# Two edits in the attention layers of a conv-attention hybrid: a product with the identity made a transpose, and four row products made one transpose and a masked product

## The chip, the cores and the metric

The kernel runs on one core of one Trainium2 chip. The metric is the device time of one execution in microseconds (us); the time given is the median of several runs. Beside the runs there is one profiled execution, whose trace gives the start and the duration of each instruction on each engine: PE is TensorE (matrix products; PEld is its separate load of the stationary operand), DVE is VectorE, ACT is ScalarE, POOL is GpSimd, SP is SyncE, which issues the DMAs.

## The reference, cut to what matters

The whole network has four layers on `x` of 2 x 56 x 56 x 128. Layers 0 and 1 are convolutions with selective scans. Layers 2 and 3 work on 2 x 3136 tokens of 128 channels: layer 2 is an attention without weights of its own and a mixer of long convolutions, layer 3 an attention with weights and 64 experts. The change touches the two attentions:

```python
def _L2_attn_ref(q):
    sim = jnp.einsum('blh,bmh->blm', q, q) * scale
    sim = jnp.where(diag[None, :, :], jnp.float32(-1000000000.0), sim)
    attn = jax.nn.softmax(sim, axis=-1)
    return jnp.einsum('blm,bmh->blh', attn, q)

def _L3_attn_ref(x, Wq, bq, Wk, bk, Wv, bv):
    q = jnp.einsum('bnf,of->bno', x, Wq) + bq
    k = jnp.einsum('bnf,of->bno', x, Wk) + bk
    v = jnp.einsum('bnf,of->bno', x, Wv) + bv
    scores = jnp.einsum('bnf,bmf->bnm', q, k) / TEMP
    alpha = jax.nn.softmax(scores, axis=-1)
    return jnp.einsum('bnm,bmf->bnf', alpha, v)

t = t + _L2_attn_ref(_ln_t(t))
t = t + _L2_ffn_ref(_ln_t(t), ...)      # the mixer
t = t + _L3_attn_ref(_ln_t(t), ...)
t = t + _L3_ffn_ref(_ln_t(t), ...)      # the experts
```

## The kernel before, in words

`program` (L2174) runs the layers one after the other: layer 0, layer 1, attention 2, the mixer, attention 3, the experts. The token tensor `X` stays in SBUF through layers 2 and 3, with 112 tokens to a partition tile.

Both attentions run in `Attend.run` (L1198). A chunk is 448 queries of one image; there are 7 chunks per image, 14 in all. A chunk goes over 25 key tiles of 128 keys (the last has 64). Per key tile `j`:

- PE forms the scores of 128 keys and 448 queries (L1219, into a PSUM pool of three banks called "sc");
- ACT takes the exponential into `e` (L1221, a pool of six);
- POOL adds `e` up in `total` (L1230, L1232), whose column sums are the softmax denominators;
- PE adds values times `e` into the accumulator `av` (L1213). This runs two key tiles behind the scores: `waiting` holds up to three tiles.

At the end of a chunk DVE copies the accumulator to `by` (L1244), channels on the partitions and 448 queries along the row. For each of four groups of 112 queries PE multiplies `by` by `out_w` (L1248), which turns the group to tokens on the partitions, and multiplies `total` by a column of ones (L1251), which gives the denominators. DVE takes the reciprocal (L1255) and adds the scaled result to `X` (L1258). In attention 3 `out_w` is the value weight matrix; in attention 2 there is no such matrix, and `out_w` is the identity. All of these are float32.

During the chunks of attention 2, `also` (L1301) puts in steps that prepare the mixer's input for the chunk before: a layernorm after tile 4 (`layernorm_tokens`, L71, on DVE, ACT and POOL), its transposes after tile 11 (L1566), and products after tiles 14 and 18 (L1578, L1595). During attention 3 it puts in the second image's layernorm, transposes and keys (L1403, L1417, L1428), and the experts' layernorm and gate products (L1930, L1934).

In attention 3 the exponent needs a shift per query, about the largest score. `Queries` (L1118) makes the next chunk's queries while the current chunk runs. `begin` (L1132), at tile 0, projects the queries into `q` and keeps a bfloat16 copy `q16`. `some` (L1146), after each tile, does two more of 28 low-precision score products (L1154, bank pool "lo" of two) and takes each one's row maximum on DVE (L1158), so that all are done by tile 15. Then it finishes:

- DVE takes the largest of seven maxima per query, negated: `m`, 112 x 4 (L1161);
- PE turns each of the four columns of `m` into a row of 112 by a product with the identity (L1164), all into one partition of one "pr" bank: 1 x 448;
- ACT copies that row to a bfloat16 row `shift` (L1169);
- PE multiplies it by `part`, one row of 1/128, which spreads the shift over the 128 channels of a second "pr" bank (L1171; the pool has one bank, so the first must be read before);
- DVE adds it to `q` (L1172).

The query vectors then carry the shift in themselves, and the next chunk's first score product needs the shifted `q` (`take`). The first chunk's queries are made ahead of the loop, in `Attention3.run` (L1348), spread over the steps that prepare the first image's keys.

The order of instructions on each engine is not written out by hand: the program is recorded in the order of the calls, and a scheduler of the language orders each engine's instructions and puts the semaphore waits. Each engine runs its own list in order.

Of the kernel before, what the change touches and what calls it, by code (L numbers as in the profile page):

```python
# [15 lines left out]
BF16 = mybir.dt.bfloat16  # L16
AF = mybir.ActivationFunctionType
ALU = mybir.AluOpType
# [7 lines left out]
TP = 112  # L26
NT = L // TP
CH = 448
# [6 lines left out]
class Chip:  # L35


    def __init__(self, ctx, tc):
        self.tc, self.nc = tc, tc.nc
        nc = tc.nc  # L40
        const = ctx.enter_context(tc.tile_pool(name="const", bufs=1))
        self.ident = const.tile([128, 128], F32, name="ident")
        make_identity(nc, self.ident)
        self.eps = const.tile([128, 1], F32, name="eps")
        nc.gpsimd.memset(self.eps, 1e-5)
        self.one = const.tile([128, 1], F32, name="one")
        nc.gpsimd.memset(self.one, 1.0)
        self.ones = const.tile([1, 128], F32, name="ones")
        nc.gpsimd.memset(self.ones, 1.0)
        self.X = const.tile([TP, NT, B, C], F32, name="X")  # L50
        self._turn = 0
# [59 lines left out]
class Scans:  # L111
# [201 lines left out]
    def run(self):  # L313
        with ExitStack() as ctx:
            self.open(ctx)
            with self.k.tc.manual_schedule():
                self.all_steps()
# [795 lines left out]
def four(ps):  # L1113

    return ps[:TP].rearrange("p (i c) -> p i c", c=C)


class Queries:  # L1118
# [6 lines left out]
    def __init__(self, k, keys, low, weights, bias, sp, banks):  # L1125
        self.k, self.keys, self.low, self.weights, self.bias, self.sp = k, keys, low, weights, bias, sp
        self.banks = banks
        self.part = sp.tile([1, 128], BF16, name="part")
        k.nc.gpsimd.memset(self.part, 1.0 / C)
        self.todo = []  # L1130

# [14 lines left out]
    def some(self, left):  # L1146

        nc = self.k.nc
        if len(self.todo) <= left:
            return  # L1150
        while len(self.todo) > left:
            c, i = self.todo.pop(0)
            ps = self.banks("lo")[:TP, 0:CH]
            nc.tensor.matmul(  # L1154
                ps, lhsT=self.q16[:, TP * i : TP * (i + 1)], rhs=self.low[self.b][:, CH * c : CH * (c + 1)],
                start=True, stop=True,
            )
            nc.vector.tensor_reduce(self.m[:, i, c : c + 1], ps, AX.X, ALU.max)  # L1158
        if not self.todo:
            m = self.sp.tile([TP, 4], F32, name="mm")  # L1160
            nc.vector.tensor_reduce(m, self.m, AX.X, ALU.max, negate=True)  # L1161
            ps = self.banks("pr")
            for i in range(4):
                nc.tensor.matmul(  # L1164
                    ps[0:1, TP * i : TP * (i + 1)], lhsT=m[:, i : i + 1], rhs=self.k.ident[:TP, :TP],
                    start=True, stop=True,
                )
            row = self.sp.tile([1, CH], BF16, name="shift")
            nc.scalar.copy(row, ps[0:1, 0:CH])  # L1169
            ps = self.banks("pr")[:, 0:CH]  # L1170
            nc.tensor.matmul(ps, lhsT=self.part, rhs=row, start=True, stop=True)  # L1171
            nc.vector.tensor_tensor(self.q, self.q, ps, ALU.add)  # L1172
# [6 lines left out]
class Attend:  # L1179
# [18 lines left out]
    def run(self, keys, queries, V, scale, out_w, skip=None, also=lambda at, j: None):  # L1198

        k, nc, X = self.k, self.k.nc, self.k.X  # L1200
        made = isinstance(queries, Queries)
        chunks = [(b, qc) for b in range(B) for qc in range(NCH)]
        for at, (b, qc) in enumerate(chunks):
            if made:
                q = queries.take()
            else:
                q = queries[b][:, CH * qc : CH * (qc + 1)]
            av = self.bank("av")
            acc = av[:, 0:CH]
            total = self.ep.tile([KT, CH], F32, name="total")  # L1210

            def weigh(j, n, e):
                nc.tensor.matmul(acc, lhsT=V[b][:n, j, :], rhs=e[:n], start=j == 0, stop=j == NKT - 1)  # L1213

            waiting, first = [], None
            for j in range(NKT):
                n = min(KT, L - KT * j)
                ps = self.bank("sc")[:, 0:CH]
                nc.tensor.matmul(ps[:n], lhsT=keys[b][:, KT * j : KT * j + n], rhs=q, start=True, stop=True)  # L1219
                e = self.sp.tile([KT, CH], F32, name="e")  # L1220
                nc.scalar.activation(e[:n], ps[:n], AF.Exp, scale=scale)  # L1221
                if skip is not None:
                    c0, c1 = max(KT * j, CH * qc), min(KT * j + n, CH * (qc + 1))
                    if c0 < c1:
                        own = e[:n, c0 - CH * qc : c1 - CH * qc]
                        nc.vector.tensor_tensor(own, own, skip[:n, c0 - KT * j : c1 - KT * j], ALU.mult)
                if j == 0:
                    first = e
                elif j == 1:
                    nc.gpsimd.tensor_tensor(total, first, e, ALU.add)  # L1230
                else:
                    nc.gpsimd.tensor_tensor(total[:n], total[:n], e[:n], ALU.add)  # L1232
                if made and at + 1 < len(chunks):
                    if j == 0:
                        queries.begin(*chunks[at + 1])
                    queries.some(max(0, 30 - 2 * j))
                waiting.append((j, n, e))
                if len(waiting) > 2:
                    weigh(*waiting.pop(0))
                also(at, j)  # L1240
            for one in waiting:
                weigh(*one)
            by = self.ep.tile([128, CH], F32, name="by")
            nc.vector.tensor_copy(by, acc)  # L1244
            pt = four(self.bank("pr"))
            pd = av[:TP, CH : CH + 4]
            for i in range(4):
                nc.tensor.matmul(  # L1248
                    pt[:, i, :], lhsT=by[:, TP * i : TP * (i + 1)], rhs=out_w, start=True, stop=True
                )  # L1250
                nc.tensor.matmul(  # L1251
                    pd[:, i : i + 1], lhsT=total[:, TP * i : TP * (i + 1)], rhs=self.ones, start=True, stop=True
                )
            r = self.ep.tile([TP, 4], F32, name="r")
            nc.vector.reciprocal(r, pd)  # L1255
            for i in range(4):
                xo = X[:, 4 * qc + i, b, :]
                nc.vector.scalar_tensor_tensor(xo, pt[:, i, :], r[:, i : i + 1], xo, ALU.mult, ALU.add)  # L1258


class Attention2:
# [30 lines left out]
    def run(self, early, inputs):  # L1292

        k = self.k
        done = early()
        with k.pool("a2") as sp, ExitStack() as ctx:
            skip = sp.tile([KT, KT], F32, name="skip")
            k.nc.vector.tensor_scalar(skip, k.ident, -1.0, 1.0, ALU.mult, ALU.add)
            att = Attend(k, ctx)

            def also(at, j):  # L1301
                steps = {4: inputs.tokens, 11: inputs.channels, 14: inputs.blocks, 18: inputs.direct}
                if at > 0 and j in steps:
                    steps[j](lambda: att.bank("lo"), *divmod(at - 1, NCH))

            att.run(self.uT, self.uT, self.V, 128.0**-0.5, k.ident, skip=skip, also=also)
            for step in (inputs.tokens, inputs.channels, inputs.blocks, inputs.direct):
                step(lambda: att.bank("lo"), B - 1, NCH - 1)
        return done
# [910 lines left out]
```

## Time and profile before

| what | us |
|---|---|
| median of 3 runs | 8835.18 |
| lowest and highest run | 8833.89, 8835.39 |
| the profiled execution: its own time | 8835.43 |
| its span, from first to last instruction | 8833.6 |
| first score product of attention 2 in its loop, last result product | 5758.4, 6360.4 |
| first tokens step of attention 3 (L1403) | 7883.8 |
| first score product of attention 3 (L1219), last result product | 7949.6, 8645.2 |

So layers 0 and 1 take the first 65% of the span, attention 2 about 600 us, the mixer about 1520, attention 3 about 760 with its preparation, the experts the last 190. Three score products of attention 2 stand earlier, at 5686, beside the end of layer 1.

How to read the views: the page's first part gives the busy time of each engine; a busy time over the whole span is a mean over stages with different limits, so stretches are asked for by themselves. A matrix product of float32 shows as two records ("x2" for one instruction of the program), a transpose and a bfloat16 product as one. In a timeline a line gives the start in us, the length in us, engine, line, operation, output and inputs, the number of records merged, and in brackets the idle time of that engine ahead of it with what ended it. In a list of waits the columns are the total in us, the times, and the longest.

### The profile page before, as it was taken

To read this page: it belongs to the slowest core of one execution; us is meant where nothing else is said; L and a number is where in the kernel's file an instruction comes from. 1 tells how busy PE (TensorE), PEld (TensorE's weight loads), DVE (VectorE), ACT (ScalarE), POOL (GpSimd) and SP (SyncE) were. 2 spreads that over 40 slices of the span, in tenths; PEclk is the share of its full clock that TensorE was granted. 3 is DMA by queue.
4 is the path that set the end of the run, shared out by engine and by line. 5 is a ranking of instruction groups with operands and counts; after the bars stand their busy time and mean duration, and the time that the engine had idled before them with its cause. 6 is when DMAs were issued, how large, how long until landed. Compare 5 with 4: busy or idle time off the path is not lost. (4 is left out here: it accounts for less than half of the span.)

```text
span 8833.6 us, 103494 instructions
## 1 busy us (share of the span) xinstructions
PE 8003.9 (91%) x31559; PEld 4877.1 (55%) x31559; DVE 6756.2 (76%) x7017; ACT 5217.6 (59%) x11166; POOL 6844.0 (77%) x4232
## 2 busy tenths in 40 slices
PE   8999999999998888888888888699989989989998
PEld 4555555555554444444444444345578878875555
DVE  8999998999987997998899799821266676665442
ACT  6888876888876776776777677533322222214331
POOL 5999986999986996998799699666577767756551
PEclk9999999999998999999899899799999999989999
DMA  4676654667654884885688488320133333320004
GB/s 145 217 218 213 211 186 128 217 217 213 211 179 109 221 219 118 215 223 161 173 224 216 116 224 219 93 34 3 30 98 106 103 93 106 104 56 8 15 1 139
DMA packets 846617, 1276.69 MB, mean 145 GB/s; under 512 B 182813, under 2 KB 504350, under 8 KB 846058
## 3 DMA queue, kind: packets, MB, share of 16 engines
q1 hardware_dynamic: 846058, 1270.07, 50.7%
q8 instruction: 249, 4.08, 0.2%
q14 instruction: 310, 2.54, 0.1%
HBM read 1230.00 MB, written 46.58 MB: 145 GB/s over the span
## 5 line engine op out<-in xcount | busy, mean ns | idle before, releaser
L495 POOL TENSOR_TENSOR p<-h,c 128x784 f32<-128x784 f32 x2048 | 3763.7, 1864 | 291.8 <-DVE h L401 146.0
L401 DVE TENSOR_TENSOR_SCAN h<-a,state,h 128x784 f32<-128x784 f32 x1200 | 2169.9, 1833 | 2.5 <-ACT a L381 1.6
L421 PE MATMUL acc<-p,center 128*128 128x392 f32 x4096 | 1496.8, 501 | 6.5 <-POOL p L495 6.3
L421 PE MATMUL acc<-p,ident 128*128 128x392 f32 x4096 | 1429.5, 493 | 0.5 <-POOL p L495 0.4
L479 DVE TENSOR_TENSOR h<-du,b 128x784 f32<-128x784 f32 x1152 | 1096.5, 952 | 229.7 <-PE b L407 212.5
L381 ACT ACTIVATE a<-delta,L1A 128x784 f32<-128x784 f32 x896 | 819.8, 915 | 425.0 <-DVE h L401 418.6
L421 PEld LDWEIGHTS acc<-p,ident 128*128 128x128 f32 x4096 | 747.6, 190 | 533.4 <-issue 33.4
L421 PEld LDWEIGHTS acc<-p,center 128*128 128x128 f32 x4096 | 743.0, 193 | 497.1 <-issue 25.0
L1232 POOL TENSOR_TENSOR total<-total,e 128x448 f32<-128x448 f32 (+1 forms) x644 | 734.6, 1141 | 329.1 <-ACT e L1221 289.6
L498 POOL TENSOR_TENSOR h<-du,b 128x784 f32<-128x784 f32 x448 | 831.7, 1857 | 0.0
L1221 ACT ACTIVATE e<-sc 128x448 f32<-128x448 f32 (+1 forms) x700 | 376.9, 542 | 722.8 <-PE sc L1219 594.6
L407 PE MATMUL b<-three,sel 96*128 96x512 bf16 (+1 forms) x2304 | 587.0, 336 | 174.0 <-DVE h L479 102.0
L381 ACT ACTIVATE a<-delta,L0A 128x784 f32<-128x784 f32 x704 | 643.3, 914 | 169.7 <-DVE h L401 165.2
L401 DVE TENSOR_TENSOR_SCAN h<-a,h 128x784 f32<-128x784 f32 x400 | 702.6, 1774 | 3.5 <-ACT a L381 3.1
L359 ACT ACTIVATE X<-X,BT 112x128 f32<-112x128 f32 x2100 | 683.8, 391 | 0.2
L1736 POOL TENSOR_TENSOR u<-u,T 128x1024 f32<-128x1024 f32 x192 | 448.6, 2358 | 265.9 <-DVE u L1734 265.7
L401 DVE TENSOR_TENSOR_SCAN h<-h,state,a 128x784 f32<-128x784 f32 x336 | 618.0, 1839 | 0.0
L1720 ACT ACTIVATE less<-cv 128x512 f32<-128x512 f32 x256 | 152.1, 595 | 612.2 <-PE cv L1698 586.9
L407 PEld LDWEIGHTS <-sel 96*128 96x128 bf16 x2304 | 225.0, 101 | 521.3 <-issue 365.5
L359 ACT ACTIVATE big<-big,BT 112x64 f32<-112x64 f32 x1680 | 444.6, 335 | 0.0
L1732 ACT ACTIVATE T<-T 128x1024 f32<-128x1024 f32 x128 | 135.2, 1056 | 407.4 <-DVE T L1730 279.2
L1837 PE MATMUL pj<-u,Wm 128*128 128x196 f32 (+8 forms) x1536 | 355.6, 385 | 21.2 <-POOL u L1756 11.1
(541 smaller groups left out, 14336.4 us busy)
## 6 DMA issues: line engine op xcount, KB each, us to landing
c<-rows SPq DMA_DIRECT2D x1024, 392.0 KB, 4.0
c<-rows SPq DMA_DIRECT2D x2048, 196.0 KB, 4.0
b<-rows SPq DMA_DIRECT2D x512, 196.0 KB, 4.6
b<-rows SPq DMA_DIRECT2D x192, 392.0 KB, 4.6
wA<-win SPq DMA_DIRECT2D x64, 448.0 KB, 3.9
wB<-win SPq DMA_DIRECT2D x64, 448.0 KB, 6.2
wC<-win SPq DMA_DIRECT2D x64, 448.0 KB, 4.7
wD<-win SPq DMA_DIRECT2D x64, 448.0 KB, 3.8
```

Of the source, the lines that this page charges most:

```text
L359: self.k.nc.scalar.activation(x["bT"][:, i, c0:c1], g["duT"][x["ci"]][:, i, c0:c1], AF.Copy, scale=g["BT"][:, r : r + 1])
L381: self.k.nc.scalar.activation(x["a"], g["delta"][ci], AF.Exp, scale=self.w["A"](g["kd"], ci, x["n"]))
L401: self.k.nc.vector.tensor_tensor_scan(h, a, b, start, ALU.mult, ALU.add)
L407: self.k.nc.tensor.matmul(ps[:, c0:c1], lhsT=self.w["selB"](x["n"]), rhs=x["g"]["three"][:, c0:c1], start=True, stop=True)
L421: nc.tensor.matmul(job["acc"][:, i, 0:392], lhsT=self.w["sum"], rhs=x["p"][:, 392 * i : 392 * (i + 1)], start=False, stop=n == NS - 1,)
L479: nc.vector.tensor_tensor(one["h"], one["g"]["du"][one["ci"]], one["b"], ALU.mult)
L495: nc.gpsimd.tensor_tensor(now["p"], now["h"], now["c"], ALU.mult)
L498: nc.gpsimd.tensor_tensor(three["h"], three["g"]["du"][three["ci"]], three["b"], ALU.mult)
L1221: nc.scalar.activation(e[:n], ps[:n], AF.Exp, scale=scale)
L1232: nc.gpsimd.tensor_tensor(total[:n], total[:n], e[:n], ALU.add)
L1736: nc.gpsimd.tensor_tensor(u[:, :, :, o], u[:, :, :, o], half, ALU.add)
L1837: nc.tensor.matmul(ps[:, lo - c0 : hi - c0], lhsT=Ws[f][:, eo, 3 - r, :], rhs=u[:, b, f, lo - a0 : hi - a0], start=f == 0, stop=f == 1,)
```

## The change

Two edits.

- In `Attend.run`, `out_w` may now be None, and attention 2 passes None instead of the identity. The result is then turned to tokens by `nc.tensor.transpose` with the identity as the moving operand, and not by a float32 product with it. Attention 3 keeps its product with the value weights.
- In `Queries.some`, the four products that lay the columns of `m` into one row become one transpose of `m` (112 x 4) into four rows of 112. One DVE tensor_tensor then multiplies these four rows, each repeated four times along the row, by the 4 x 4 corner of the identity, each element repeated 112 times. The result `shift` is 4 x 448 in bfloat16: row `i` holds its own 112 values at place `i` and zeros elsewhere. `part` gets four rows of 1/128 instead of one, so the spreading product (now with four partitions instead of one) adds the four rows up to the same 448 values. ACT's copy is gone.

```diff
@@ class Queries: __init__
-        self.part = sp.tile([1, 128], BF16, name="part")
+        self.part = sp.tile([4, 128], BF16, name="part")
         k.nc.gpsimd.memset(self.part, 1.0 / C)
@@ Queries.some
             m = self.sp.tile([TP, 4], F32, name="mm")
             nc.vector.tensor_reduce(m, self.m, AX.X, ALU.max, negate=True)
-            ps = self.banks("pr")
-            for i in range(4):
-                nc.tensor.matmul(
-                    ps[0:1, TP * i : TP * (i + 1)], lhsT=m[:, i : i + 1], rhs=self.k.ident[:TP, :TP],
-                    start=True, stop=True,
-                )
-            row = self.sp.tile([1, CH], BF16, name="shift")
-            nc.scalar.copy(row, ps[0:1, 0:CH])
+            ps = self.banks("pr")[0:4, 0:TP]
+            nc.tensor.transpose(ps, m, self.k.ident[:TP, :TP])
+            row = self.sp.tile([4, CH], BF16, name="shift")
+            shape = [4, 4, TP]
+            nc.vector.tensor_tensor(
+                row.rearrange("p (i c) -> p i c", c=TP), ps.unsqueeze(1).to_broadcast(shape),
+                self.k.ident[0:4, 0:4].unsqueeze(2).to_broadcast(shape), ALU.mult,
+            )
             ps = self.banks("pr")[:, 0:CH]
             nc.tensor.matmul(ps, lhsT=self.part, rhs=row, start=True, stop=True)
             nc.vector.tensor_tensor(self.q, self.q, ps, ALU.add)
@@ Attend.run
             for i in range(4):
-                nc.tensor.matmul(
-                    pt[:, i, :], lhsT=by[:, TP * i : TP * (i + 1)], rhs=out_w, start=True, stop=True
-                )
+                if out_w is None:
+                    nc.tensor.transpose(pt[:, i, :], by[:, TP * i : TP * (i + 1)], k.ident)
+                else:
+                    nc.tensor.matmul(
+                        pt[:, i, :], lhsT=by[:, TP * i : TP * (i + 1)], rhs=out_w, start=True, stop=True
+                    )
                 nc.tensor.matmul(
                     pd[:, i : i + 1], lhsT=total[:, TP * i : TP * (i + 1)], rhs=self.ones, start=True, stop=True
                 )
@@ Attention2.run
-            att.run(self.uT, self.uT, self.V, 128.0**-0.5, k.ident, skip=skip, also=also)
+            att.run(self.uT, self.uT, self.V, 128.0**-0.5, None, skip=skip, also=also)
```

Line numbers from L1162 on are up to three higher in the changed kernel.

## The prediction

> **What bounds the kernel now.** I read the page's first part, then busy time by stretch, then TensorE's waits, then the timeline at the two places that the diff touches. The page puts TensorE first, and the stretches say where that matters: attention 2 lies at 5759 to 6361 us, the loop of attention 3 at 7949 to 8646.
>
> ```profile
> PE 8003.9 (91%) x31559; PEld 4877.1 (55%) x31559; DVE 6756.2 (76%) x7017; ACT 5217.6 (59%) x11166; POOL 6844.0 (77%) x4232
> ...
> core 0: us, PE busy (x) PEld busy (x) DVE busy (x) ACT busy (x) POOL busy (x), PEclk, DMA share, GB/s
> 5759.00:6361.00 602.00, 601.13 (x1830) 311.18 (x1828) 106.96 (x249) 236.19 (x423) 395.92 (x349) 1.00 0.06 11
> 7949.00:8303.00 354.00, 347.17 (x1174) 180.32 (x1173) 184.06 (x343) 155.38 (x254) 214.75 (x193) 1.00 0.03 10
> 8306.00:8646.00 340.00, 337.92 (x1106) 174.89 (x1104) 146.34 (x283) 130.49 (x222) 200.15 (x177) 1.00 0.01 5
> ```
>
> In both stretches PE is busy 98 to 100% at the full granted clock (1.00), DMA is nearly idle, and no other engine passes 66%. TensorE's waits inside attention 3's loop say the same:
>
> ```profile
> PE lo L1154 <- DVE m L1158: 6.8, 21, 0.6
> PE pr L1248 <- DVE by L1244: 0.7, 1, 0.7
> PE pr L1417 <- POOL U L86: 0.5, 3, 0.2
> ```
>
> A PE microsecond here is therefore a microsecond of the end, if nothing else becomes late. In the timeline, take distances between starts of weight loads, since ends of matmuls are modelled. The end of an attention 2 chunk:
>
> ```profile
> 5798.74 0.28 PEld L1248 LDWEIGHTS pr<-ident,by 128*112 128x112 f32 x2
> 5798.95 0.29 PEld L1251 LDWEIGHTS av<-onecol,total 128*112 128x112 f32 x2
> 5799.16 0.28 PEld L1248 LDWEIGHTS pr<-ident,by 128*112 128x112 f32 x2
> ```
>
> Each float32 product is two passes ("x2"): 0.21 us for a result product, 0.21 for a row-sum product, 0.42 for a pair. A float32 transpose of the same shape already stands in the kernel, at L1403, and is one pass; four of them take 8028.92 to 8029.36, 0.11 us each:
>
> ```profile
> 8028.92 0.60 PE L1403 MATMUL pr<-ident,A 128*112 128x128 f32 x4
> 8029.25 0.30 PEld L1219 LDWEIGHTS sc<-q,first 128*128 128x128 f32 x2
> 8029.36 0.92 PE L1219 MATMUL sc<-q,first 128*128 128x448 f32 x2
> ```
>
> And the maxima of a later chunk of attention 3: eight passes, a value product, the spreading product L1171, DVE's addition.
>
> ```profile
> 8142.18 0.18 DVE L1161 TENSOR_REDUCE mm<-m 112x4 f32<-112x28 f32 x1
> 8142.57 0.66 PEld L1164 LDWEIGHTS pr<-ident,mm 112*1 112x1 f32 x8 [0.65 <-issue]
> 8143.43 0.30 PEld L1213 LDWEIGHTS av<-e,first 128*128 128x128 f32 x2 [0.20 <-ACT e L1221]
> 8143.53 0.52 ACT L1169 CAST shift<-pr 1x448 bf16<-1x448 f32 x1 [0.25 <-PE pr L1164]
> 8144.38 0.09 PEld L1171 LDWEIGHTS <-part 1*128 1x128 bf16 x1 [0.65 <-issue]
> 8144.78 0.62 DVE L1172 TENSOR_TENSOR q<-q,pr 128x448 f32<-128x448 f32 x1 [2.42 <-PE pr L1171]
> ```
>
> From 8142.57 to 8143.43 is 0.86 us for eight passes, 0.107 each.
>
> **What the Trainium skill says.** "TensorE: Matmul & The Clock Gate", section Terms, calls the transpose mode four times faster for float32. This trace shows only half the time (0.11 against 0.21), and I use the trace. "Perfetto Trace Analysis", section Transposes, advises a transpose instead of a standard matmul; the same rows agree. "VectorE: DVE Perf Modes", section on the TRN2 errata, prices a float32 tensor_tensor at (N+151)/0.96 ns, 624 ns for 448 elements; L1172 with 448 elements and one operand in PSUM took 621, so it agrees. The TensorE page's Part 1 says that the PE runs at half clock until a window of about 3.4 us has been busy; here the stretch 7940 to 7946 shows a granted clock of 0.50, and 7948 to 7950 shows 1.00.
>
> **The change part by part.**
>
> *Attention 2's results (14 chunks, 4 each).* Each product of two passes (0.21) becomes one transposed pass of L1403's shape (0.11): 0.10 saved, 4 x 14 x 0.10 = 5.6 us. Bounds: nothing, if the alternation with the row sums sets the pace; 5.9, if the pass costs as little as half the pair, 0.105. The addition to the tokens waits for the row sums, which come after the same passes, so the normalization and the next steps on DVE, ACT and POOL start 0.4 us earlier too: nothing takes PE's place as the late one. `total` was complete at 5796.14, 2.4 us before its product.
>
> *Attention 3's maxima, 13 times in the loop.* Four products (eight passes, 0.86 us) become one transpose with 4 stationary columns and 112 moving ones. The nearest rows are the transposes with 112 moving columns (L1566: 6247.46 to 6247.85, four, 0.10 each). Saved 0.86 - 0.10 = 0.76 us; 13 x 0.76 = 9.9 us. Bounds: 8.6, if the single transpose takes 0.2, and 10.4, if it takes 0.06.
>
> *ACT's copy of the row goes to DVE.* ACT loses 14 x 0.52 us; ACT is 38 to 44% busy in the loop, so I count nothing. DVE gains 14 tensor_tensor of 4x448 with an operand in PSUM: 0.62 each by L1172. Bounds 0.47 (448 elements with no fixed part) and 2.0 (four cycles an element, if the two broadcasts slow it). What hides it: in the built order of the changed program, L1171 stands after a value and a score product (2 x 0.75 us) in every chunk of the loop; in the later chunks it stood after one before. The row needs 0.11 (PE's end to DVE's start, as at L1172) + 0.62 + 0.21 (DVE's mm end 8142.36 to L1164's start 8142.57) = 0.94 us. So L1171 does not wait, by 0.56 us. If the cover were gone, it would cost 0.94 x 13 = 12 us. Behind a waiting L1171 on PE stand the next score and value products; behind the row on DVE stand the reciprocal L84 and the addition L1172. In the chunks with a normalization in flight (three of the loop) L84 waits for ACT's root, which ends at 8036.90 in the second of them, while the row would run at about 8035.7 to 8036.3: nothing. `U` is then complete at 8038.29 and its transpose L1417 comes at 8039.78 now, 0.76 earlier after: still 0.7 us to spare.
>
> *The first maxima, ahead of the loop.* Here the chain is exposed and the PE clock is half: L1164 from 7946.40, ACT's copy from 7947.97, L1171 from 7948.54, the addition from 7948.93, first score product 7949.60. After: one pass, done by about 7946.75; DVE's row 7946.85 to 7947.47; its cast of q (0.39) to 7947.86, L1171 meanwhile; addition from about 7948.0 to 7948.6; score product 7948.65, some 0.95 earlier. One low-precision score product (0.19) moves from ahead of it to behind it. I take 0.7. Bounds: 1.0, and a loss of 1.0, if the thinner PE work leaves the clock at half for one more window (3.4 us at half speed is 1.7 lost).
>
> *Moves without a price.* In the seventh chunk of attention 2 the built order puts the first L1566 transpose five tiles earlier, just where PE stands still for an exponential (6067.27 to 6067.52); its input is done at 6066.94. Zero, at most 0.3. `part` gets three more rows: one memset. SP's queue is untouched.
>
> Sum: 5.6 + 9.9 + 0.7 = 16.2 us. The profiled execution took 8835.43 (span 8833.6 and 1.8 around it): 8835.4 - 16.2 = 8819.2. The median is 0.25 lower, so 8819.0, 0.18% less. About 0.2% (17.7 us) is what a measurement of this kernel can tell from no change, so the forecast is a real gain that just misses it.
>
> **The rivals.**
> - *More than counted* (8816): each L1164 and L1171 also shows some 0.1 to 0.2 us between the end of the passes before it and its own first pass, because its load was not pulled ahead. If one of these goes per chunk, 13 x 0.2 = 2.6 us more. For it: the row is ready half a microsecond before L1171's turn, so its load may go ahead. Against it: the load stood exposed before as well, though the copy was done 0.3 us earlier.
> - *The transposes of results gain nothing* (8824.6): the pace of 0.104 per pass is as near to a weight load of 112 columns as to a stream of 128, and alternating modes may cost what the pass saves. Against it: L1403 and L1566 stand between normal products with no gap over 0.03 us.
> - *Attention 3's gain turns into waits* (8829, only 5.6 + 0.7 left): PE comes 0.76 us earlier to exponentials or to `U`. Against it: value products lag by two tiles, and the spare time above.
> - *Slower, by the row on DVE* (8841): the row of 4x448 with two stride-0 operands takes d. Above d = 1.2 us (1.5 less 0.32) L1171 stops PE at all 13 places, and from d = 2.4 (16.2/13 more) the whole change loses. At d = 2.85, 13 x 1.65 = 21.5 lost, less 16.2, is +5. Against it: broadcast operands in L80 (512 elements, 0.69) run at an element per cycle.
>
> **How the numbers follow.** Forecast as summed, 8817 to 8821.5: 0.62. More than counted: 0.18. No gain in attention 2: 0.08. Waits: 0.08. Slower: 0.04. The range 8814 to 8826 takes in the first three with their bounds (0.88, of which some spills over). Faster by over 0.2% (below 8817.5): the second case and a tail of the first, 0.25. Slower by over 0.2% would need d of about 3.8 us or an unforeseen stall: 0.03. Within: 0.72.
>
> **What would show it.** In the profile after: L1248's line in attention 2 with 56 records instead of 112 and 0.32 us from pair to pair; one record in place of L1164's eight and 0.1 us between its load and the next product's; a DVE row of about 0.62 us and no PE wait on it; the stretches of attention 2 and of the loop of attention 3 shorter by 5.6 and 9.9 us, others as before. PE waiting at L1171 for DVE, or a row above 1.2 us, would show it wrong; so would mixer or expert stages that change length.

## The result and the profile after

The changed kernel takes 8815.5 us (median of 12 runs, 8808.65 to 8821.97), the kernel before 8834.42 in the same comparison (12 runs, 8825.94 to 8845.55): a ratio of 0.9979 [0.9972, 0.9987] (in brackets, here and below, a 95% interval), 18.9 us less. The forecast was 16.2 us less, 8819.0.

The profiled execution of the changed kernel was the longest of its twelve, 8821.97 us with a span of 8820.2. Its span is only 13.4 us shorter than the profiled span before, so spans must be compared by stage. The stages below are cut at starts of products that both programs have: first value product of attention 2, last row sum of attention 2, first tokens step of attention 3 (L1403, now L1406), first and last score product of attention 3's loop, end of the span.

| stage, us | before | after | difference |
|---|---|---|---|
| up to attention 2 | 5760.1 | 5758.3 | -1.8 |
| attention 2 | 600.6 | 592.8 | -7.8 |
| mixer | 1523.5 | 1524.1 | +0.6 |
| attention 3, preparation | 65.4 | 64.7 | -0.7 |
| attention 3, loop | 690.4 | 680.0 | -10.4 |
| experts, end | 193.6 | 200.3 | +6.7 |

The three stages with an edit in them got 18.9 us shorter. The experts got 6.7 longer though nothing in them was edited, which was not expected and is taken up below.

First the same views as before. The page's first part and the busy time of the stretches of the changed kernel (attention 2, and the two halves of attention 3's loop; after the comma the busy time and records of PE, PEld, DVE, ACT, POOL, then the granted clock):

```profile
PE 7989.4 (91%) x31405; PEld 4864.6 (55%) x31405; DVE 6764.6 (77%) x7031; ACT 5212.6 (59%) x11152; POOL 6843.2 (78%) x4232
```

```profile
core 0: us, PE busy (x) PEld busy (x) DVE busy (x) ACT busy (x) POOL busy (x), PEclk, DMA share, GB/s
5757.40:6350.80 593.40, 592.68 (x1769) 302.41 (x1768) 106.96 (x247) 236.34 (x423) 396.68 (x349) 1.00 0.07 11
7939.89:8280.00 340.11, 333.52 (x1104) 173.19 (x1104) 188.45 (x350) 147.93 (x240) 209.23 (x188) 1.00 0.03 8
8280.00:8619.90 339.90, 338.81 (x1070) 174.01 (x1069) 148.89 (x283) 130.67 (x222) 205.87 (x182) 1.00 0.02 7
```

PE has 154 records fewer: 56 in attention 2 and 14 times seven in attention 3. DVE has 14 more, ACT 14 fewer. PE is still busy 98 to 100% of the three stretches, and no other engine took its place. TensorE's waits in attention 3's loop are those of before, to the tenth of a microsecond:

```profile
PE lo L1154 <- DVE m L1158: 6.8, 21, 0.6
PE pr L1251 <- DVE by L1244: 0.7, 1, 0.7
PE pr L1420 <- POOL U L86: 0.5, 3, 0.2
```

There is no wait at the spreading product (L1171) for DVE's new row. The three new groups, by line (duration in ns: least, median, most):

```profile
L1249 PEld LDWEIGHTS pr<-ident,by x56: 132/203/207, 5796.4 to 6350.8; 128*112 128x112 f32 x56
...
L1163 PE MATMUL pr<-ident,mm x14: 256/256/391, 7937.6 to 8566.3; 112*4 112x112 f32 x14
...
L1166 DVE TENSOR_TENSOR shift<-pr,ident x14: 612/612/614, 7938.0 to 8566.6; 4x448 bf16<-4x448 f32 x14
```

The row on DVE takes 612 ns, the same each time. The end of an attention 2 chunk, in the weight loads of the changed kernel:

```profile
5796.44 0.14 PEld L1249 LDWEIGHTS pr<-ident,by 128*112 128x112 f32 x1 [0.19 <-issue]
...
5796.95 0.21 PEld L1249 LDWEIGHTS pr<-ident,by 128*112 128x112 f32 x1
5797.05 0.32 PEld L1254 LDWEIGHTS av<-onecol,total 128*112 128x112 f32 x2
5797.22 0.20 PEld L1249 LDWEIGHTS pr<-ident,by 128*112 128x112 f32 x1
5797.31 0.31 PEld L1254 LDWEIGHTS av<-onecol,total 128*112 128x112 f32 x2
5797.48 0.20 PEld L1249 LDWEIGHTS pr<-ident,by 128*112 128x112 f32 x1
...
5797.81 0.30 PEld L1219 LDWEIGHTS sc<-big 128*128 128x128 f32 x2
```

From transpose to transpose it is 0.27, 0.26 us (5796.95, 5797.22, 5797.48), where a pair took 0.42. From the first load of the block to the load of the next score product it is 1.37 us; before it was 1.94:

```profile
5798.05 0.18 PEld L1248 LDWEIGHTS pr<-ident,by 128*112 128x112 f32 x1 [0.19 <-issue]
...
5799.99 0.30 PEld L1219 LDWEIGHTS sc<-big 128*128 128x128 f32 x2
```

That is 0.57 less per chunk, and 14 x 0.57 = 8.0, which is the stage's difference to 0.2 us.

The maxima of a chunk of attention 3, PE's records. Before:

```profile
8141.73 0.92 PE L1219 MATMUL sc<-q,first 128*128 128x448 f32 x2
8142.57 0.93 PE L1164 MATMUL pr<-ident,mm 112*1 112x112 f32 x8
8143.43 1.02 PE L1213 MATMUL av<-e,first 128*128 128x448 f32 x2
```

After, with DVE's row and the spreading product in another view of the same stretch:

```profile
8130.78 0.92 PE L1219 MATMUL sc<-q,first 128*128 128x448 f32 x2
8131.56 0.26 PE L1163 MATMUL pr<-ident,mm 112*4 112x112 f32 x1
8131.65 0.93 PE L1213 MATMUL av<-e,first 128*128 128x448 f32 x2
```

```profile
8131.85 0.61 DVE L1166 TENSOR_TENSOR shift<-pr,ident 4x448 bf16<-4x448 f32 x1 [0.44 <-PE pr L1163]
8132.42 0.92 PE L1219 MATMUL sc<-q,first 128*128 128x448 f32 x2
8133.26 0.09 PEld L1171 LDWEIGHTS <-part 4*128 4x128 bf16 x1 [0.65 <-issue]
```

From the start of the score product to the end of the value product behind the block it was 2.72 us (8141.73 to 8144.45) and is 1.80 (8130.78 to 8132.58): 0.92 less, against a forecast of 0.76. The row is done at 8132.46, and L1171 comes 0.8 us later. DVE is off PE's path.

Last, the start of the loop. Before, its first two score products (four passes) took 1.77 us:

```profile
7949.60 1.77 PE L1219 MATMUL sc<-q,first 128*128 128x448 f32 x4 [0.28 <-DVE q L1172]
```

After, the same four passes:

```profile
7939.89 3.20 PE L1219 MATMUL sc<-q,first 128*128 128x448 f32 x4
```

They run at half clock: the changed kernel enters the loop before TensorE's clock has come up, and gives back 3.20 - 1.77 = 1.43 us inside the loop.

### The profile page after: what moved, and what is told of

It reads as the page before. It is cut to its first block, busy times and chain, and to the rows that moved or that the text cites. A ratio compares the mean times of both kernels' runs of the same rounds, so it can differ in the third digit from the quotient of the medians.

```text
span 8820.2 us, 103186 instructions
## 1 busy us (share of the span) xinstructions
PE 7989.4 (91%) x31405; PEld 4864.6 (55%) x31405; DVE 6764.6 (77%) x7031; ACT 5212.6 (59%) x11152; POOL 6843.2 (78%) x4232
## 6 DMA issues: line engine op xcount, KB each, us to landing
c<-rows SPq DMA_DIRECT2D x2048, 196.0 KB, 4.1
b<-rows SPq DMA_DIRECT2D x512, 196.0 KB, 4.6
```

## The experiments

Four questions were open: whether the two edits act only in their own stages; why the end got 6.7 us longer; why a pair in attention 2 fell by 0.15 us where the price taken gave 0.10; and why a block in attention 3 fell by 0.92 where 0.76 was counted. All kernels were compared with the kernel before on the same chip. Their stages:

| stage, us | attention 2 | preparation | loop | end |
|---|---|---|---|---|
| before | 600.6 | 65.4 | 690.4 | 193.6 |
| after | 592.8 | 64.7 | 680.0 | 200.3 |
| attention 2's edit alone | 592.7 | 65.7 | 690.5 | 200.3 |
| attention 3's edit alone | 601.0 | 64.7 | 679.9 | 194.9 |
| the change again | 592.3 | 64.6 | 680.0 | 194.9 |
| transposes grouped | 594.4 | 64.7 | 680.0 | 194.8 |
| four transposes in attention 3 | 593.1 | 65.5 | 683.5 | 200.0 |
| row made three times | 592.4 | 66.8 | 680.3 | 193.3 |
| extra products at the end | 592.5 | 64.6 | 680.1 | 196.0 |
| extra products in two places | 593.2 | 65.4 | 678.6 | 195.0 |

In the grouped kernel the last row sums stand eight passes in a row, and its stage is cut at the last of them. The expectations of attention 2's edit alone, attention 3's edit alone, the change again and the grouped kernel count attention 2 from its first score product, 1.6 us ahead of the first value product: their 602.2 us are 600.6 in this table, and their 594.4, 596.6 and 597.2 are 592.8, 595.0 and 595.6.

### Attention 2's edit alone

The kernel before, with `out_w` None in attention 2.

```diff
-                nc.tensor.matmul(
-                    pt[:, i, :], lhsT=by[:, TP * i : TP * (i + 1)], rhs=out_w, start=True, stop=True
-                )
+                if out_w is None:
+                    nc.tensor.transpose(pt[:, i, :], by[:, TP * i : TP * (i + 1)], k.ident)
...
-            att.run(self.uT, self.uT, self.V, 128.0**-0.5, k.ident, skip=skip, also=also)
+            att.run(self.uT, self.uT, self.V, 128.0**-0.5, None, skip=skip, also=also)
```

> Attention 2's edit alone (results turned by transposes); attention 3's maxima as before. Theory T (a transposed pass costs about 0.05 us of PE when it stands between normal passes, a quarter of the two passes of the product, so a pair falls from 0.415 to 0.264 us): attention 2 from its first loop score product to its last row sum takes 594.4 us instead of 602.2, and the loop of attention 3 stays at 690.4. The whole kernel is 7.8 us faster than before, give or take the clock of the experts' start. Rival P (the prediction's size, 0.10 us saved per result): 596.6 us and 5.6 us.

Measured: 8831.53 us (13 runs, 8827.92 to 8841.52), ratio 0.9997 [0.9989, 1.0005]. Attention 2 took 592.7, the loop 690.5, the end 200.3. The stage falls by 7.9, which is theory T's size and not the prediction's (592.8 and 595.0 in the table's cut), and no other edited stage moves. Theory T's size was worked out after the first profile, so this repeats a measurement; it doesn't show what a single transposed pass costs. The interval of the whole (7 us to either side) can't tell 8 us from nothing; the stage can.

### Attention 3's edit alone

The changed kernel, with the identity back as attention 2's `out_w`.

```diff
-            att.run(self.uT, self.uT, self.V, 128.0**-0.5, None, skip=skip, also=also)
+            att.run(self.uT, self.uT, self.V, 128.0**-0.5, k.ident, skip=skip, also=also)
```

> Attention 3's edit alone; attention 2 turns its results by products with the identity as before. Theory T: attention 2 stays at 602.2 us; in attention 3 a chunk of the loop is 0.91 us shorter (the row maxima cost PE 0.14 us instead of 1.06), 13 x 0.91 = 11.9 us, so the loop from first to last score product takes 678.5 us if the PE clock is full at its start and 680.0 if it is at half there. Rival P: 0.76 us a chunk, 680.5 and 682. Whole kernel 11 to 12 us faster than before. If the two edits act on each other, this and attention 2's edit alone don't sum to the change.

Measured: 8828.9 us (8819.77 to 8847.62), ratio 0.9994 [0.9986, 1.0002]. Attention 2 601.0, preparation 64.7, loop 679.9, end 194.9. Each edit moves its own stage by what the two together move it; by stage the parts add up (7.9 + 0.7 + 10.5 = 19.1). The medians of the whole (4 and 7 us) don't, and their intervals don't ask them to.

### The change again

The changed kernel, not edited.

> The changed kernel again, nothing edited, for its spread. Theory C (which window the PE clock gate opens in decides the stage after the loop of attention 3): attention 2 594.4 us and the loop 678.5 to 680.0 as in the first profile, but the end from the last score product on anywhere from 193 to 201 us, with the difference lying wholly in PE passes at half clock in its first 60 us. Rival D (the change itself makes the end longer, 200 instead of 194 us): again 200 us.

Measured: 8813.45 us (7 runs, 8808.28 to 8818.29), ratio 0.9975 [0.9964, 0.9986]. The edited stages repeat to half a microsecond (attention 2 begins while the clock is still coming up: its first four value passes took 3.19 us in one profile and 2.97 in the other), and the end is 194.9 instead of 200.3, from the same program. So the 6.7 us belong to the execution and not to the change. The clock shows it. Busy time by stretch, two windows of 30 us from the last score product on. The changed kernel's first profile:

```profile
core 0: us, PE busy (x) PEld busy (x) DVE busy (x) ACT busy (x) POOL busy (x), PEclk, DMA share, GB/s
8619.90:8649.90 30.00, 14.57 (x60) 10.20 (x58) 15.18 (x31) 7.66 (x8) 6.39 (x6) 0.59 0.71 245
8649.90:8679.90 30.00, 28.57 (x159) 21.00 (x160) 5.23 (x15) 0.70 (x2) 2.66 (x1) 0.78 0.00 1
```

The same kernel again:

```profile
8615.80:8645.80 30.00, 14.20 (x72) 9.96 (x71) 15.09 (x31) 7.66 (x8) 6.36 (x6) 0.66 0.69 245
8645.80:8675.80 30.00, 28.56 (x184) 20.38 (x184) 5.91 (x16) 1.83 (x4) 2.66 (x1) 0.94 0.01 1
```

The kernel before:

```profile
8640.00:8670.00 30.00, 14.57 (x69) 10.25 (x67) 15.18 (x31) 7.66 (x8) 6.34 (x6) 0.66 0.67 245
8670.00:8700.00 30.00, 28.56 (x193) 21.15 (x192) 6.29 (x20) 2.17 (x6) 2.66 (x1) 1.00 0.00 1
```

PE is busy 28.6 of 30 us in every second window, but at a clock of 0.78, 0.94 or 1.00 it gets through 159, 184 or 193 records, and the end takes 200.3, 194.9 or 193.6. In the first window PE waits a good half of the time, and from there the clock comes back at different moments. Of the kernels without extra products, those with a clock of 0.78 to 0.80 in that window ended in 200.0 to 200.3, those with 0.94 in 194.8 to 194.9, those with 1.00 in 193.3 to 193.6. Of the kernel before there is one profile only, so an effect of about a microsecond on the end can't be ruled out.

### The transposes grouped, apart from the row sums

The changed kernel, with the four transposes (and, in attention 3, the four products) in one loop and the four row sums in a second.

```diff
+            for i in range(4):
                 nc.tensor.matmul(
                     pd[:, i : i + 1], lhsT=total[:, TP * i : TP * (i + 1)], rhs=self.ones, start=True, stop=True
```

> The changed kernel, but in attention 2 and 3 the four result products or transposes of a chunk stand first and the four row-sum products after them, instead of alternating. Theory T (the transposed pass is short, but a row of transposes is paced by the loads of 112 columns, 0.10 to 0.11 us each, while between row sums, which stream one column, passes and loads fill each other's gaps): four transposes 0.43 us and four row sums 0.83, 1.26 instead of 1.06 us a chunk; attention 2 is 14 x 0.2 = 2.8 us longer, 597.2 us. Rival (a transposed pass costs 0.055 us wherever it stands): 594.4 us.

Measured: 8817.85 us (8807.9 to 8830.21), ratio 0.9981 [0.9973, 0.9989]; attention 2 594.4. The weight loads of the end of a chunk:

```profile
5793.82 0.13 PEld L1249 LDWEIGHTS pr<-ident,by 128*112 128x112 f32 x1 [0.19 <-issue]
5794.19 0.35 PEld L1249 LDWEIGHTS pr<-ident,by 128*112 128x112 f32 x3 [0.24 <-issue]
5794.52 0.88 PEld L1255 LDWEIGHTS av<-onecol,total 128*112 128x112 f32 x8
5795.31 0.30 PEld L1219 LDWEIGHTS sc<-big 128*128 128x128 f32 x2
```

Three transposes in a row take 0.33 us, 0.11 each, and eight row-sum passes 0.79, 0.099 each: near the prices that the prediction used. The block takes 1.49 us, 0.45 less than before, and alternated it takes 0.12 less again. So a transposed pass is no cheaper than the price; three passes that alternate are: 0.27 for three is 0.09 each. Over 14 chunks the 0.12 come to 1.7 us; the stage is 1.2 to 2.1 us longer than in the seven kernels that alternate (592.3 to 593.2). The direction is shown; the expected size for alternating, 0.2 a chunk, was too large.

Attention 3's blocks of the same kernel are a control. There the four products with the value weights and the four row sums were taken apart too, and all of them are two passes. A block takes 1.94 us grouped (8193.79 to 8195.73) and 1.94 alternated in the changed kernel (8196.60 to 8198.54). So the order matters where transposes are among the passes, and not where all are products. Seven product passes in a row take 0.76 us there, 0.11 each: next to its like, a product takes 0.22 and not 0.21, so that four transposes in a row save 0.44, which is the grouped block's 0.45. Why loads and passes fit together more tightly when the modes alternate is not shown here.

### Four transposes instead of one in attention 3

The kernel before with attention 2's edit, and each of the four columns of maxima turned into its row by a transpose of its own; ACT's copy and the one-row `part` stay.

```diff
-                nc.tensor.matmul(
-                    ps[0:1, TP * i : TP * (i + 1)], lhsT=m[:, i : i + 1], rhs=self.k.ident[:TP, :TP],
-                    start=True, stop=True,
-                )
+                nc.tensor.transpose(ps[0:1, TP * i : TP * (i + 1)], m[:, i : i + 1], self.k.ident[:TP, :TP])
```

> The changed kernel, but attention 3's maxima come as four transposes of one column each into one row, with ACT's copy and one row of 1/128 as before the change: it shares the transposes with the change and not the masked product. It measures a transposed pass whose weight load is one column. Theory T1 (a transposed pass streams 112 columns in about a quarter of the two passes of a product, 0.05 us): four take 0.2 us, so a chunk of the loop is 0.65 to 0.75 us shorter than before, and the loop from first to last score product takes 681.5 us. Rival T2 (a pass is a pass, 0.10 us, and the change gains by having one instead of eight): four take 0.43 us, the loop takes 684.5 us. Attention 2 from its first value product to its last row sum as in the changed kernel, 592.5 us.

Measured: 8827.22 us (8816.19 to 8842.51), ratio 0.999 [0.9982, 0.9998]; loop 683.5. PE around a block:

```profile
8135.82 0.92 PE L1216 MATMUL sc<-q,first 128*128 128x448 f32 x2
8136.60 0.54 PE L1164 MATMUL pr<-ident,mm 112*1 112x112 f32 x4
8136.98 0.93 PE L1210 MATMUL av<-e,first 128*128 128x448 f32 x2
8137.84 0.36 PE L1168 MATMUL pr<-shift,part 1*128 1x448 bf16 x1
```

Score start to value end is 2.09 us here (8135.82 to 8137.91), 1.80 with one transpose, 2.72 with eight passes. Three passes more than one cost 0.29, 0.097 each: a pass of a small transpose is worth 0.10, not 0.05. Over 13 blocks that is 3.8 us, and the loop is 3.5 longer than the changed kernel's; at its start this kernel lost 0.4 us less to the clock (its first four passes took 2.79 us). Taken apart by starts, the three programs read:

| us | before | four transposes | one transpose |
|---|---|---|---|
| score product's start to the block's | 0.84 | 0.78 | 0.78 |
| block's start to the value product's | 0.86 | 0.38 | 0.09 |
| the value product's length | 1.02 | 0.93 | 0.93 |

The block itself saves 0.77, what was forecast. The other 0.15 lies at its two edges: 0.06 ahead of the first pass, and 0.09 in the value product behind. Ends of products are modelled, but the starts agree: from the value product to the spreading product behind it is 0.95 before (8143.43 to 8144.38) and 0.86 with four transposes (8136.98 to 8137.84). The value product's weights are loaded from its own start on in the kernel before (8143.43), and from 0.09 to 0.10 ahead of it in the other two (8136.88, 8131.56). Both edges are gone with four transposes already, and one transpose gains nothing more there. So they go with the eight product passes; whether by their kind or by their number, no run separates.

### The row on DVE made three times

The changed kernel, with the masked product written three times into the same row.

```diff
+            for _ in range(3):
+                nc.vector.tensor_tensor(
+                    row.rearrange("p (i c) -> p i c", c=TP), ps.unsqueeze(1).to_broadcast(shape),
+                    self.k.ident[0:4, 0:4].unsqueeze(2).to_broadcast(shape), ALU.mult,
+                )
```

> The changed kernel with the masked product on DVE written three times over the same row (two of them superfluous): 1.84 instead of 0.61 us from the transpose to the row. In the built order the spreading product stands three products after the transpose (2.25 us) instead of two, so the scheduler has moved it on its own. Theory H (the row is hidden, and the order follows its length): 2.2 us of chain against 2.25 of cover, the loop of attention 3 stays within 1 us of 680.0, and only the stretch ahead of the loop gets 1.0 to 1.3 us longer, 66 instead of 64.7. Rival S (the row is on the path of every chunk, as in the prediction's slow case): 13 x 1.2 us, the loop takes 695.

Measured: 8818.48 us (8810.35 to 8824.25), ratio 0.9983 [0.9975, 0.999]; loop 680.3, preparation 66.8. In the loop, 26 further rows of 0.61 us on DVE cost 0.3 us: the order built for this program has L1172 (the spreading product) one product later, and PE's list of waits shows none on DVE's row. It is close: in one chunk the third row ends at 8129.13, a quarter of a microsecond ahead of the load of L1172 at 8129.38. The work is hidden because the scheduler keeps it hidden. Ahead of the loop nothing hides it:

```profile
7930.92 0.61 DVE L1167 TENSOR_TENSOR shift<-pr,ident 4x448 bf16<-4x448 f32 x1 [1.21 <-PE pr L1163]
7931.76 0.61 DVE L1167 TENSOR_TENSOR shift<-pr,ident 4x448 bf16<-4x448 f32 x1
...
7933.09 0.60 DVE L1167 TENSOR_TENSOR shift<-pr,ident 4x448 bf16<-4x448 f32 x1
7933.75 0.10 PEld L1172 LDWEIGHTS <-part 4*128 4x128 bf16 x1 [1.22 <-DVE shift L1167]
```

The three rows stand over 2.8 us with other DVE work between them, PE waits 1.22 us at L1172, and the preparation is 2.1 us longer than with one row, more than was expected.

### Extra products ahead of the experts

A try at keeping the clock up: the changed kernel with twelve products that nothing reads, six before the last gate step and six before the experts' selection.

```diff
+            warm = att.bank("lo")[:TP, 0 : 3 * C]
+            for i in range(6):
+                k.nc.tensor.matmul(
+                    warm, lhsT=k.ident[:TP, :TP], rhs=k.X[:, NT - 4 : NT - 1, B - 1, :], start=True, stop=True
+                )
             experts.tokens(self.sp, B - 1, NCH - 1)
...
+                warm = gp.tile([128, CH], F32, name="warm")
+                for i in range(6):
+                    nc.tensor.matmul(warm, lhsT=k.ident, rhs=pr[:, L - CH :], start=True, stop=True)
```

> The changed kernel with twelve superfluous float32 products that nothing reads: six after attention 3's last addition to the tokens and six after the last gate row, where PE stands idle for 7 us each time. They leave the result as it is. Theory C (the end from the last score product on is 194 or 200 us by the clock gate's windows): PE stays at full clock, the granted clock of the first 60 us after the last score product rises from 0.66 and 0.8 to 0.94 to 1.00 in both halves, and the end takes 190 to 192 us every time; the kernel gains 3 to 9 us. Rival (other waits set the end's length): 194 to 200 as before, or more by the products themselves.

Measured: 8819.37 us (8810.29 to 8836.73), ratio 0.9983 [0.9976, 0.9989]; end 196.0. The aim was a clock near 1.00; it was 0.88 in the first 30 us and 0.89 in the second. PE after the last row sum:

```profile
8617.96 0.27 PE L1254 MATMUL av<-onecol,total 128*112 128x1 f32 x2
8619.41 6.83 PE L1398 MATMUL lo<-X,ident 112*112 112x384 f32 x12 [1.18 <-DVE X L1261]
8626.08 0.55 PE L1938 MATMUL pr<-ident,U 112*128 112x112 f32 x4
...
8629.08 4.78 PE L1983 MATMUL warm<-pr,ident 128*128 128x448 f32 x12 [0.72 <-ACT pr L1943]
8635.47 2.00 PE L2002 MATMUL ps<-shares,sel 128*112 128x128 f32 x16 [1.61 <-DVE shares L1993]
8639.28 4.66 PE L2010 MATMUL sum<-selT,X 112*128 112x64 f32 x32 [1.81 <-DVE selT L2007]
8643.74 3.70 PE L2002 MATMUL ps<-shares,sel 128*112 128x128 f32 x16
```

The first twelve passes stand after 1.18 us of idle PE and take 6.83 us, 0.57 each for 384 columns, where a pass of 448 columns takes 0.375 at full clock: most of them ran at half clock. The gate transposes behind them come 13.6 us after the last score product instead of 12.5. The second twelve (8629.08) take 0.40 each for 448 columns, near full speed. But at 8643.74 sixteen passes of L2002 take 3.70 us, where sixteen took 2.00 at 8635.47: the granted clock was 1.00 up to 8641.0, 0.83 in the next 1.5 us and 0.50 from 8642.5 on. It fell inside a stretch without a gap (from 8639.28 on), after PE had stood still for 1.61 and 1.81 us. The idea fails: the end took 196.0, not 190 to 192. In the kernels without extra products the end's length goes with the clock of the second window, but these products don't hold the clock; what decides the windows stays open.

### Extra products there and in attention 3's preparation

The kernel of the section before, with three products that nothing reads after each of the first six preparation steps.

```diff
+                warm = att.bank("pr")[:, 0:CH]
+                for i in range(3 if c + 1 < NCH else 0):
+                    k.nc.tensor.matmul(
+                        warm, lhsT=k.ident, rhs=self.uT[0][:, CH * c : CH * (c + 1)], start=True, stop=True
+                    )
```

> As the run before, and three more superfluous float32 products after each of the first six steps that prepare attention 3's first image, where PE is at half clock. Theory C: the clock there rises to 1.00, the preparation falls from 64.7 us to about 60, and the loop starts at full clock: 678.3 instead of 680.0. Rival: the products stand in front of the chain of the next step on PE, and the preparation gets longer by up to 18 x 0.4 us.

Measured: 8821.81 us (8806.63 to 8829.07), ratio 0.9983 [0.9976, 0.999]; preparation 65.4, loop 678.6. Here the clock is up when the loop starts:

```profile
7938.82 0.34 PE L1171 MATMUL pr<-shift,part 4*128 4x448 bf16 x1 [0.70 <-DVE shift L1166]
...
7939.88 1.77 PE L1219 MATMUL sc<-q,first 128*128 128x448 f32 x4
```

The granted clock is 1.00 in twelve microseconds ahead of the loop, where it was 0.50. The four passes take 1.77 us as before the change, and the loop is 1.4 shorter than the changed kernel's. Now the loop has no clock loss, and its saving is 690.4 - 678.6 = 11.8, which over 13 blocks is 0.91, the 0.92 read from a single block. The preparation takes 0.8 more than in the kernel of the section before, and not the 60 us expected, though the clock was up: its length doesn't hang on the clock alone. So the two stages together gain about 0.7 us: not enough to see in the whole, and no version here beats the changed kernel by more than its runs vary.

## Why the prediction was right, and where its terms were off

The mechanism was right. PE was the bound in both stretches, a PE microsecond saved was a microsecond of the end, and nothing else became late: 16.2 us were forecast, 18.9 measured by the medians, 19.2 as the sum of the stages over the profiles (attention 2 8.1, from means with and without the edit; preparation 0.7; loop 10.4). The 2.7 us between forecast and medians are less than the spread of the runs; what can be judged is the terms.

- *Attention 2's results, 4 x 14 x 0.10 = 5.6, bounds 0 to 5.9: too small, the upper bound too.* Measured 7.4 to 8.7 (600.6 and 601.0 without the edit; 592.3 to 593.2 in the seven kernels that alternate). From pair to pair it is 0.27 us, where 0.32 was forecast. The prices were right where they were taken from (0.11 for a transpose in a row, 0.10 for a row-sum pass, both repeated in the grouped kernel). The step that failed is that these prices were added for passes that alternate. In the alternated block three passes take 0.26 to 0.27 us. The surplus is 0.17 a chunk. 0.12 of it is alternation, shown by the grouped kernel; the other 0.05 is the product's price, 0.21 as read among row sums and 0.22 next to its like, four times. The rival that expected alternation to eat the saving had the sign wrong.
- *Attention 3's maxima, 13 x (0.86 - 0.10) = 9.9: the block was mis-sized.* It saves 0.92. The distance of 0.86 ran from the first pass to the next product, and that part fell by 0.77 as forecast; left out was what stood exposed ahead of the first pass and behind the last, 0.15. The rival "more than counted" came near in size: 13 x 0.2 = 2.6, where 13 x 0.15 = 2.0 came. In place it was right by less than half: it named the gap ahead of the block (0.06) and not the product behind (0.09). It named L1171 as a second place; there the load stands exposed after as before (8133.26, with 0.65 us of idle ahead of it, the same figure as before).
- *The row on DVE: priced at 0.62 and hidden.* 0.612, and no wait. The rival "slower by the row on DVE" began from a row of 1.2 us; even three rows, 1.84 us in sum, cost the loop 0.3 us, because the order of PE was built anew around them. The rival's premise, a fixed place for L1171, was wrong.
- *Ahead of the loop: -0.7, with -1.0 to +1.0.* The preparation did get 0.7 shorter. The loss named as the lower bound came as well, the clock staying at half for one more window: 1.43 us at the loop's first products. Together this step lost 0.7 us. In all six profiles with attention 3's edit and no extra products in the preparation, some twelve microseconds ahead of the loop showed a clock of 0.50; in the two without the edit they showed 0.56 and 0.58, the clock coming up just at the end. With four transposes in place of eight passes it was 0.50 as well. The Trainium skill, "TensorE: Matmul & The Clock Gate", Part 4, says that transposes don't count as busy work for the clock. Here eight passes became one transpose, or four, so less work and another kind came together, and no run separates them.
- *The moves without a price, and ACT's freed copy: nothing.* The mixer's length differs by 0.6 us from before, and over all the kernels it lay between 1522.2 and 1524.5; the blocks' 8.0 us leave next to nothing of attention 2's 8.1 for the move in the seventh chunk.

So the misses were +2.5 (attention 2), +2.0 (the edges of the blocks) and -1.4 (clock), 3.1 in all; the forecast fell short of the stages' sum by 3.0. It had named the last two, near their sizes, as a rival and as a bound. That one of the three has the other sign brought the sum nearer to the measurement, and that is luck.

The end of the kernel is the term that nobody had: 193 to 200 us in unchanged code, with the clock. The prediction had named an experts' stage of another length as a sign of being wrong; it came, and the change run again showed that it was none. The end moves the time of a single execution by a third of the change's whole effect. The stages up to attention 2, unchanged too, move it more: over the ten profiles they took 5751.5 to 5761.8 us. "TensorE: Matmul & The Clock Gate", Part 1, says that the clock's window runs free and doesn't start with the kernel; the two profiles of one program, 200.3 and 194.9, are in keeping with that and don't show it.

## What to carry to other kernels

A product with the identity in float32 is two passes and a transpose is one, and many small products into one partition can become one transpose; count a block from the work ahead of it to the work behind it, since what stands exposed at its edges can go with it. Where PE was the bound, work put on an engine with room cost nothing, and the scheduler's order moved to keep it so; ahead of the loop nothing hid it. An effect of 0.1% in one stage is read from that stage's length, cut at products that both programs have, and not from the whole, where the clock of another stage can outweigh it.

## What the runs showed of the hardware that was not expected

- A float32 transpose of 112 stationary and 128 moving columns takes 0.11 us when transposes follow each other. Alternated with two-pass products, a transposed and two product passes take 0.26 to 0.27 us, less than the sum of the prices in a row (0.11 + 2 x 0.099 = 0.31). Four products and four row sums, all of two passes, take 1.94 us in either order.
- A DVE product of 4x448 with one operand in PSUM and both operands spread by broadcasts takes 0.612 us, no more than a plain one of 128x448 (0.62).
- Twelve passes issued to keep the clock up ran mostly at half clock themselves after 1.2 us of idle PE (0.57 us each). In the same profile the clock fell from 1.00 to 0.50 between 8641.0 and 8642.5, inside a stretch without a gap, after idle gaps of no more than 1.81 us.
